# Where the magnitudes of a soft threshold lie: two PSUM banks for them, or a third pair of banks for the inverse beside them

## The chip, the cores and the metric

One core of a Trainium2 chip runs the whole program in one launch. The metric is the device time in microseconds, median of several runs; a profile of one execution stands beside it. The engines are TensorE (PE, with its weight loads as PEld), VectorE (DVE), ScalarE (ACT), GpSimd (POOL) and SyncE (SP), which issues the DMAs. Each engine works through its own queue in order.

## The reference

Four layers work on images x of shape (4, 64, 256, 256): batch, channels, rows, columns.

```python
# layers 0, 2 and 3: a long convolution with an implicit, separable filter
k_f = jnp.fft.rfft2(k, s=(512, 512)) / 512      # k = outer product of hx and hy, per channel
y = jnp.fft.irfft2(jnp.fft.rfft2(x, s=(512, 512)) * k_f, s=(512, 512))[..., :256, :256]
x = y + x * bias[:, None, None]
# layer 1: mixing of channels in the Haar domain, with a soft threshold
f1 = haar2d(x)
for i in range(2):
    f4 = jnp.einsum('bchw,oc->bohw', f1 * v[i], conv_w[i])
    acc = acc + jnp.sign(f4) * jax.nn.relu(jnp.abs(f4) - tau[i])
x = haar2d(acc, inverse=True) + x
```

The change is in layer 1's soft threshold: `jnp.abs(f4)` is the magnitude, `jnp.abs(f4) - tau` and the product with the sign are two VectorE operations on it.

## The kernel before

**Tiling.** The convolutions are done as products with Toeplitz matrices, rows first and then columns, in 64x64 tiles of TensorE (`toeplitz`, L337, its matmuls at L341). The Haar transform is partly a matmul with a 64x64 matrix (`haar`, L350, matmuls at L353) and partly sums and differences on GpSimd (`forward_free` and `inverse_free`, L430). The batch is cut in two groups of two images. A round t is a group and two channels; there are 32 rounds in a group and 64 in all.

**Stages.** `phase_a` does layer 0 and the forward transform. `phase_b(grp)` is the mixing of one group: for each of 64 steps two units u, one for each of the two terms i. `phase_c` does the inverse transform and layers 2 and 3. The order is written out by hand: each phase is a list of pieces, and `beside(main, side, ...)` (L1017) issues the pieces of one list spread evenly over those of another. The first mixing (group 0) goes beside `phase_a`'s second half, the second mixing (group 1) beside `phase_c`'s first 29 rounds; the rest of `phase_c`, the last stage, runs alone. The engines keep the order in which the pieces were issued, and semaphores settle the rest.

**A unit of the mixing** (L732): `mix` (L654) multiplies into the PSUM tile f4, named f in the profile; `multiply` (L673, DVE) takes it times v into the SBUF tile x; `sign` (L679, ACT) gives m; `magnitude` (L688, ACT) the absolute value; `less` (L693, DVE) subtracts the threshold; `threshold` (L698, DVE) takes the larger of that and 0 times the sign; `add` (L713 to L717, POOL) sums up into gt. In the second mixing every second unit from step 2 on is "raw": `multiply` only copies f4 out (L670) and the last stage's `shrink` (L829 to L855) thresholds it there.

**A round of the inverse** (`phase_c`'s `piece`, L950) has 18 pieces: rows of layer 2 (c1r), an inverse product (c0ps), columns of layer 3 of two rounds back (c2c), rows of layer 3 of the round before (c2r), another product (c0ps), columns of layer 2 (c1c). Each of them multiplies into a pair of PSUM banks from `banks` (L138), which goes around the list `rings`; a pair of the rows and columns serves two pieces, a pair of the product one. ACT copies c1r, c2r (L914) and c0ps (L902) out, DVE copies c1c and c2c with the residual (L933). These copies are issued by `flush` at the start of the piece that follows.

**PSUM** has 8 banks. In the first mixing: `acps` 4 (two pairs), f4 2, magnitude a 2. In the second mixing: `acps` 4, `wide2` 2 (a third pair), f4 2, while the magnitude overwrites x in SBUF. In the last stage: `acps` 4, `wide2` 2, the shrink tile x 2.

Of the kernel before, what the change touches and what calls it, by code (L numbers as in the profile page):

```python
# [41 lines left out]
F32 = mybir.dt.float32  # L42
AF = mybir.ActivationFunctionType
ALU = mybir.AluOpType
PSUM = bass.MemoryType.PSUM
DRAM = bass.MemoryType.DRAM

P = 128
# [19 lines left out]
GROUPS = 2  # L68
NB = B // GROUPS
# [15 lines left out]
W = 2 * N  # L85
# [16 lines left out]
def conv_haar_kernel(  # L102
# [19 lines left out]
    def pool(name, bufs, stack=ctx, **kw):  # L122
        return stack.enter_context(tc.tile_pool(name=name, bufs=bufs, reuse_waits="tile", **kw))

    ac = pool("ac", 2)
    acps = pool("acps", 4, space=PSUM)
# [8 lines left out]
    rings = [acps]  # L135
# [433 lines left out]
    def phase_b(grp):  # L569
# [4 lines left out]
        def raw(u):  # L574
            return grp == GROUPS - 1 and u % 2 == 1 and FULL <= u // 2 < STEPS
        st = [dict() for _ in range(STEPS)]
        un = [dict() for _ in range(units)]
# [103 lines left out]
        def magnitude(u):  # L681
            if raw(u):
                return
            if grp == GROUPS - 1:
                un[u]["a"] = un[u]["x"]
            else:
                un[u]["a"] = bps.tile([P, NB, W], F32, tag="a", name=f"a_{grp}_{u}", bufs=1)
            nc.scalar.activation(un[u]["a"], un[u]["x"], AF.Abs)  # L688

        def less(u):  # L690
# [41 lines left out]
        def piece(u, j):  # L732
# [13 lines left out]
            elif j == 1:  # L746
                if 0 < u <= units and grp < GROUPS - 1:
                    less(u - 1)
                if u + 1 < units and grp < GROUPS - 1:
                    mix(u + 1)  # L750
                if u < units:
                    sign(u)
                if i and s < STEPS and grp == GROUPS - 1:
                    store_raw(s)
                if 0 < u <= units:
                    threshold(u - 1)
                if i == 0 and s > 0:

                    load_v(s + 2)
                    if grp < GROUPS - 1:  # L760
                        load_f(s + 3)
            else:
                if u + 1 < units and grp == GROUPS - 1:
                    mix(u + 1)
                if i and s > 0 and grp == GROUPS - 1:
                    load_f(s + 3)
                if u < units:
                    magnitude(u)
                if i == 0 and s < STEPS:
                    exchange(s)  # L770
# [246 lines left out]
    def beside(main, side, lead, tail, weights=(1,)):  # L1017


        weights = [weights[k % len(weights)] for k in range(len(main))]  # L1020
        all_of = sum(weights[lead : len(main) - tail])
        done = 0
        for k, p in enumerate(main):
            p()
            want = len(side) * sum(weights[lead : k + 1]) // max(1, all_of)
            for q in side[done:want]:
                q()
            done = max(done, want)
# [10 lines left out]
    bps = pool("bps", 2, during, space=PSUM)  # L1039
# [3 lines left out]
    a = a[-2 * A_PIECES :]  # L1043
# [5 lines left out]
    beside(a_last[:1] + c_loads[1:] + a_last[1:] + c_first + a_end[:1], c_sums[half_way:], 2, 3)  # L1049
    during.close()  # L1050
    bp = pool("b2", 2, during)
    rings[:] = [acps, acps, pool("wide2", 2, space=PSUM)]
    bps = pool("bps2", 2, during, space=PSUM)

    main = c[:BLOCKS] + c[mid:C_PIECES] + a_end[1:] + c[BLOCKS:mid] + c[C_PIECES:cut_c]
    beside(main, phase_b(1), len(a_end) - 1 + 2 * BLOCKS, 0)
    during.close()
    late["sb"] = pool("late", 1)
    late["ps"] = pool("late_ps", 1, space=PSUM)
    beside(c[cut_c:], [], 0, 0)  # L1060
# [123 lines left out]
```

## Time and profile before

| what | before |
|---|---|
| median of three runs | 2478.4 us (2474.0 to 2486.93) |
| the profiled execution | 2475.7 us, span 2473.9 us |
| busy: PE, PEld, DVE, ACT, POOL | 91%, 76%, 72%, 56%, 84% of the span |
| first mixing, matmuls of L654 | 414 to about 1000 us |
| second mixing, matmuls of L654 | 1085 to 1762 us |
| last stage, alone | about 1770 us to the end |

A line of the groups view gives line, engine, operation, out<-in, shapes and count, then total busy time in us and the mean of one in ns, then the idle time of the engine just before them and what ended it. A line of the waits view gives who waited for whom: us in total, times, longest. A line of the timeline gives start and duration in us, engine, line and operation. A line of the table by stage gives the stretch and its length, then the busy time of PE, PEld, DVE, ACT and POOL with their instructions, the granted PE clock, the share of DMA and GB/s.

### The profile page before, as it was taken

What the parts mean: (1) busy time and instruction counts of PE and PEld (TensorE: products, weight loads), DVE (VectorE), ACT (ScalarE), POOL (GpSimd) and SP (SyncE); (2) the same over time, 40 slices, a digit from 0 to 9 for tenths busy, and PEclk for the clock granted to TensorE, in tenths of its full rate; (3) what the DMA queues carried; (4) which work ended last, traced back from release to release, by engine and by line L of the source; (5) the groups of instructions that cost most, each with busy time, mean ns of one, the idle gap of its engine ahead of it and who ended that gap; (6) DMA issues with size and microseconds to landing.
All of it is one profiled execution on the core that took longest, in us unless ns stands there. A gap on an engine that the chain in (4) does not pass through costs nothing.

```text
span 2473.9 us, 119298 instructions
## 1 busy us (share of the span) xinstructions
PE 2260.7 (91%) x53298; PEld 1883.8 (76%) x53298; DVE 1791.3 (72%) x1959; ACT 1392.7 (56%) x2318; POOL 2066.2 (84%) x2412
## 2 busy tenths in 40 slices
PE   7999998777777777778999999999999999999999
PEld 5779997444444444556887878888899999999998
DVE  4533335999999999768777777777577777777763
ACT  1232223677777777355666666666565555655552
POOL 2988887899999999777877878777889999999990
PEclk9999999999999999888999999999999999999999
DMA  6788888899999999557999999998866666666642
GB/s 198 246 279 303 295 306 302 285 350 354 359 336 359 354 344 338 208 200 276 328 316 327 330 326 334 334 334 312 282 221 218 211 214 212 218 215 212 219 166 102
DMA packets 222969, 688.03 MB, mean 278 GB/s; under 512 B 31470, under 2 KB 32815, under 8 KB 218232
## 3 DMA queue, kind: packets, MB, share of 16 engines
q1 hardware_dynamic: 222456, 680.40, 78.5%
q8 instruction: 419, 6.86, 1.1%
q14 instruction: 94, 0.77, 0.1%
HBM read 428.16 MB, written 252.12 MB: 275 GB/s over the span
## 4 chain that ended last, share of the span: by engine, by line
PE 46%; DVE 4%; DMA 2%; ACT 2%; issue 1%; SPq 1%; DVEq 0%; ACTq 0%
PE c2c L341 10%; PE c2r L341 10%; PE c1c L341 10%; PE c1r L341 9%; PE c0ps L353 4%; PE f L654 4%; DMA g<-mixed 1%; DVE x L693 1%; DVE cy L933 1%; DVE m L698 1%; DMA toep<-filt 1%; DVE x L673 1%; DMA rows<-in_v_rows 0%; ACT ch L914 0%; DVE o L933 0%
## 5 line engine op out<-in xcount | busy, mean ns | idle before, releaser
L430 POOL TENSOR_TENSOR i<-i,g 128x16 f32<-128x16 f32 x744 | 442.8, 616 | 27.2
L654 PE MATMUL f<-ft,mix 64*64 64x512 f32 x2048 | 306.8, 616 | 123.8 <-DVE x L673 109.4
L341 PEld LDWEIGHTS a2ps<-toep,ay 64*64 64x64 f32 x8192 | 303.7, 136 | 117.1 <-DVE f L522 53.2
L341 PE MATMUL a2ps<-toep,ay 64*64 64x128 f32 (+3 forms) x8192 | 336.9, 303 | 24.0 <-DVE f L522 20.6
L341 PEld LDWEIGHTS c1c<-toep,ch 64*64 64x64 f32 x8192 | 315.8, 133 | 42.9 <-issue 10.5
L341 PEld LDWEIGHTS c2c<-toep,ch 64*64 64x64 f32 x8192 | 306.5, 133 | 42.8 <-issue 12.5
L341 PEld LDWEIGHTS a1ps<-toep,x 64*64 64x64 f32 x8192 | 284.3, 134 | 58.9 <-issue 34.0
L341 PE MATMUL c1c<-toep,ch 64*64 64x256 f32 (+3 forms) x8192 | 323.0, 297 | 5.5 <-ACT ch L914 3.3
L341 PEld LDWEIGHTS c2r<-toep,cy 64*64 64x64 f32 x8192 | 300.8, 134 | 27.6 <-issue 13.9
L341 PE MATMUL c2r<-toep,cy 64*64 64x256 f32 (+3 forms) x8192 | 317.5, 297 | 4.4 <-issue 4.0
L341 PE MATMUL c1r<-toep,z 64*64 64x256 f32 (+3 forms) x8192 | 316.4, 297 | 5.4 <-issue 3.4
L430 POOL TENSOR_TENSOR ci<-i,g 128x1024 f32<-128x1024 f32 x124 | 315.7, 2566 | 4.5
L341 PE MATMUL a1ps<-toep,x 64*64 64x128 f32 (+3 forms) x8192 | 314.2, 298 | 5.7 <-DMA toep<-filt 2.4
L341 PEld LDWEIGHTS c1r<-toep,z 64*64 64x64 f32 x8192 | 298.3, 133 | 27.5 <-issue 11.2
L341 PE MATMUL c2c<-toep,ch 64*64 64x256 f32 (+3 forms) x8192 | 315.7, 297 | 3.0 <-issue 2.6
L679 ACT ACTIVATE m<-x 128x1024 f32<-128x1024 f32 x194 | 206.0, 1062 | 160.3 <-DVE x L673 122.1
L716 POOL TENSOR_TENSOR gt<-m,ft 128x512 f32<-128x512 f32 x128 | 164.5, 1285 | 152.7 <-DVE m L698 135.4
L489 ACT COPY ay<-a1ps 128x512 f32<-128x512 f32 x256 | 137.3, 589 | 269.2 <-PE a1ps L341 268.6
L914 ACT COPY ch<-c2r 128x512 f32<-128x512 f32 x256 | 137.2, 590 | 255.0 <-PE c2r L341 254.7
L673 DVE TENSOR_TENSOR x<-f,v 128x1024 f32<-128x1024 f32 x192 | 233.4, 1215 | 30.8 <-PE f L654 29.8
L509 DVE SCALAR_TENSOR_TENSOR x<-x,bias_sb,a2ps 128x512 f32<-128x512 f32 x256 | 179.5, 742 | 92.6 <-POOL f L391 51.3
L914 ACT COPY ch<-c1r 128x512 f32<-128x512 f32 x256 | 137.5, 594 | 167.1 <-PE c1r L341 166.7
(86 smaller groups left out, 3992.7 us busy)
## 6 DMA issues: line engine op xcount, KB each, us to landing
toep<-filt SPq DMA_DIRECT2D x768, 112.0 KB
ft<-coef SPq DMA_DIRECT2D x128, 512.0 KB
mixed<-gt SPq DMA_DIRECT2D x128, 512.0 KB
g<-mixed SPq DMA_DIRECT2D x256, 256.0 KB
x<-in_x SPq DMA_DIRECT2D x128, 256.0 KB
coef<-f SPq DMA_DIRECT2D x128, 256.0 KB
x<-in_x SPq DMA_DIRECT2D x32, 1024.0 KB
v<-in_v SPq DMA_DIRECT2D x64, 512.0 KB
```

Source lines behind the costliest of these rows:

```text
L341: nc.tensor.matmul(ps[r][half(c), j % 2, k * ROW :], data[half(r), c, k, bass.ts(j, ROW)], t(r, c)[:, : N - k * ROW], start=k == 0, stop=k ...
L353: nc.tensor.matmul(ps[r][half(c)].rearrange("p h k -> p (h k)"), matrix[half(r)], pairs(r, c).rearrange("p h k -> p (h k)"), start=True, s ...
L430: engine.tensor_tensor(to, s, d, op)
L489: later(lambda y=y, ps=ps: nc.scalar.copy(y, ps))
L509: nc.vector.scalar_tensor_tensor(to, old, bias_sb[:, c : c + 1], ps, ALU.mult, ALU.add)
L654: nc.tensor.matmul(un[u]["f4"][half(q), b, :], mixers[0][half(r), bass.ts(i, C)], st[s]["f"][half(r), b], start=True, stop=True, tile_posi ...
L673: nc.vector.tensor_tensor(un[u]["x"], un[u]["f4"], both(u, "v"), ALU.mult)
L679: nc.scalar.activation(un[u]["m"], un[u]["x"], AF.Sign)
L693: nc.vector.tensor_tensor(un[u]["a"], un[u]["a"], both(u, "tau"), ALU.subtract)
L698: nc.vector.scalar_tensor_tensor(un[u]["m"], un[u]["a"], 0.0, un[u]["m"], ALU.max, ALU.mult)
L716: nc.gpsimd.tensor_tensor(g[:, 0], m[:, 0], st[s]["f"][:, 0], ALU.add)
L914: later(lambda y=y, ps=ps: nc.scalar.copy(y, ps))
```

## The change

The magnitude of the second mixing is written to a PSUM tile `a` of its own, with one buffer, as in the first mixing. Its two banks are those of `wide2`: the inverse's ring has only `acps` (two pairs) while the second mixing runs, and gets `wide2` once the mixing's pools are closed, when the last stage begins.

```diff
         def magnitude(u):
             if raw(u):
                 return
-            if grp == GROUPS - 1:
-                un[u]["a"] = un[u]["x"]
-            else:
-                un[u]["a"] = bps.tile([P, NB, W], F32, tag="a", name=f"a_{grp}_{u}", bufs=1)
+            un[u]["a"] = bps.tile([P, NB, W], F32, tag="a", name=f"a_{grp}_{u}", bufs=1)
             nc.scalar.activation(un[u]["a"], un[u]["x"], AF.Abs)
...
     during.close()
     bp = pool("b2", 2, during)
-    rings[:] = [acps, acps, pool("wide2", 2, space=PSUM)]
     bps = pool("bps2", 2, during, space=PSUM)

     main = c[:BLOCKS] + c[mid:C_PIECES] + a_end[1:] + c[BLOCKS:mid] + c[C_PIECES:cut_c]
     beside(main, phase_b(1), len(a_end) - 1 + 2 * BLOCKS, 0)
     during.close()
+    rings[:] = [acps, acps, pool("wide2", 2, space=PSUM)]
     late["sb"] = pool("late", 1)
```

## The prediction

> **What bounds the kernel now.** I read the page first (TensorE, PE, 91% busy), then the table by stage, because the change touches one stage only: the second mixing, which runs beside the first rounds of the inverse (group 0). The matmuls of the mixing (L654) begin at 1085 us and end at 1762; the inverse starts at about 1053.
>
> ```profile
> 1053.00:1085.00 32.00, 20.70 (x412) 13.76 (x412) 17.42 (x23) 13.07 (x29) 30.36 (x47) 0.88 0.62 221
> 1085.00:1150.00 65.00, 55.07 (x1134) 41.94 (x1138) 53.90 (x47) 37.60 (x62) 43.82 (x38) 0.87 0.61 205
> 1150.00:1770.00 620.00, 602.27 (x14278) 516.88 (x14274) 459.31 (x439) 410.98 (x719) 479.85 (x522) 1.00 0.92 325
> 1770.00:2474.00 704.00, 694.33 (x18983) 658.83 (x18975) 483.55 (x548) 384.39 (x728) 596.60 (x598) 1.00 0.61 203
> ```
>
> The columns are length, then busy time of PE, weight loads, VectorE (DVE), ScalarE (ACT) and GpSimd (POOL), clock, DMA share, GB/s. In 1150 to 1770, PE is busy 602 of 620 us (97%), DVE 74%, ACT 66%, POOL 77%. So **PE sets the pace**: time freed on DVE or POOL is worth only what it takes out of PE's few gaps, and a new stall of PE counts in full. Next I asked what PE still waits for from 1053 to 1770, and the waits view names these as the largest that another engine causes (matmuls first, then weight loads; single waits of the start-up, for ft and cy, left out):
>
> ```profile
> PE f L654 <- DVE x L673: 8.4, 8, 1.6
> PE c1c L341 <- ACT ch L914: 3.3, 2, 3.0
> ...
> PEld f L654 <- DVE x L673: 11.3, 8, 3.1
> PEld c1c L341 <- ACT ch L914: 6.4, 10, 3.1
> PEld c2c L341 <- ACT ch L914: 4.3, 10, 0.8
> ```
>
> Weight load and matmul wait together, so the two kinds of rows overlap and I do not add them: about 11 us for f4 and 11 for the copies (6.4 + 4.3). Waits named "issue", some 54 us of weight-load waits in the same stretch (12.2, 11.6, 9.8, 9.6, 9.0, 2.2), have no releaser in the profile; I leave them alone. What DVE loses shows in the groups of the mixing, first the second mixing (1085 to 1770), then the first (410 to 1000):
>
> ```profile
> L698 DVE SCALAR_TENSOR_TENSOR m<-x,m 128x1024 f32<-128x1024 f32 x66 | 107.6, 1630 | 4.9
> L693 DVE TENSOR_TENSOR x<-x,v 128x1024 f32<-128x1024 f32 x64 | 98.1, 1533 | 7.8 <-ACT x L688 7.5
> ```
>
> ```profile
> L693 DVE TENSOR_TENSOR a<-a,v 128x1024 f32<-128x1024 f32 x128 | 157.1, 1227 | 7.2 <-ACT a L688 7.2
> L698 DVE SCALAR_TENSOR_TENSOR m<-a,m 128x1024 f32<-128x1024 f32 x127 | 155.5, 1225 | 14.2 <-DVE a L693 0.5 <-POOL f L391 0.5
> ```
>
> Same operations, same shapes: 1630 and 1533 ns with the magnitude in SBUF, 1225 and 1227 with it in PSUM.
>
> **What the Trainium skill says.** "SBUF — State Buffer", section "SBUF: two separate sides": VectorE and GpSimd share a port pair under an exclusive lock; a VectorE operation with two SBUF inputs and a GpSimd operation that reads SBUF shut each other out for a whole instruction. The trace agrees: only the rows with two SBUF inputs are stretched. "ScalarE: Activation LUTs", section "Step-by-step: what each stage is for": ScalarE writes PSUM faster than SBUF; L688 has a median of 1028 ns into PSUM and 1059 into SBUF. "VectorE: DVE Perf Modes", section "The perf-mode tier table (the rule you actually need)": an fp32 tensor_tensor runs at 1x from SBUF as from PSUM, so the PSUM operand itself should cost nothing; the shortest L693 in SBUF is 1207 ns, against 1227 on average in PSUM. "PSUM — Partial Sum Buffer", section "Terms": 8 banks of 2 KiB. A magnitude tile of 2 x 512 fp32 is 4 KiB, two banks, just what the third pair holds.
>
> **Part 1, the magnitude in PSUM.** 66 L698, 64 L693, and two L693 listed separately (4.8 us) fall to 1225: 107.6 + 98.1 + 4.8 - 132 x 1.225 = 49 us less on DVE. The 66 L688 save 66 x 31 ns = 2 us on ACT. No instruction is added, no DMA moves, SP's and POOL's queues keep their order. POOL loses the opposite waits: ci<-i,g took 2755 ns on average here, 2387 at its median over the kernel, so 54 x 0.37 = 20 us on this group alone. None of this lies on the path except through PE's 22 us of waits above. POOL is waited for by PE for under 2 us. From both sides: the gain is 0 to 22 us; I take **10**, since about half of those waits have a stretched instruction ahead of them at most.
>
> One wait is added: the magnitude tile has one buffer, so ACT's Abs of one shrunk unit waits until DVE's threshold of the shrunk unit before it. Behind it on ACT stand the exchange copies and the inverse's copies. From the third step on every second unit is not shrunk, so four side pieces, at 384 side pieces in 685 us some 7 us, lie between: no wait. Only the first four units are shrunk one after the other; the first mixing shows that case (L688 waits for m L698 114.5 us, 80 times, 1.4 each): at most 4 x 1.4 = 6 us, at a start-up where ACT waits for DVE anyway. I take 0.
>
> **Part 2, two pairs instead of three.** A round of the inverse uses ten pairs of banks: c1r, c1r, c0ps, c2c, c2c, c2r, c2r, c0ps, c1c, c1c. Today a pair is needed again three pairs later, then two. The rule I read off the timeline: is the last copy out of pair k-2 over when the first matmul of pair k starts today? One stretch, with all three engines:
>
> ```profile
> 1432.04 1.13 PE L353 MATMUL c0ps<-ci,inverse_sb 64*64 64x512 f32 x8
> 1432.90 3.50 PE L341 MATMUL c1c<-toep,ch 64*64 64x256 f32 x91
> 1433.50 6.80 POOL L430 TENSOR_TENSOR ci<-i,g 128x1024 f32<-128x1024 f32 x2
> 1434.08 1.07 ACT L914 COPY ch<-c2r 128x512 f32<-128x512 f32 x2
> 1434.85 3.21 DVE L698 SCALAR_TENSOR_TENSOR m<-x,m 128x1024 f32<-128x1024 f32 x1
> 1437.98 2.71 DVE L933 SCALAR_TENSOR_TENSOR cy<-z,bias_sb,c1c 128x512 f32<-128x512 f32 x4
> 1438.12 0.38 PE L341 MATMUL c1r<-toep,z 64*64 64x256 f32 x1
> ```
>
> c1c starts at 1432.90; the second c2r pair, two before it with only the 1.1 us inverse product between, is emptied by 1434.08 + 1.07 = 1435.15: 2.25 us late. c1r starts at 1438.12; the first c1c pair is empty only after two of the four cy copies, 1437.98 + 1.4 = 1439.4: 1.3 late. The second delay has a stretched threshold ahead of it (3.21 instead of 1.22); the first has not, it is ACT's queue.
>
> Done for every pair: from 1150 to 1770, 100 of 253 are late, 125.8 us in all: c2r to c1c 34.0, c1c to c1r 30.6, c1r to c2c 25.9, c0ps to c2c 11.2, c0ps to c1c 10.7, c2c to c2r 7.2, c1r to c0ps 5.9, rest 0.3. From 1053 to 1150, 18 of 32, 30.5 us. A delay shifts what follows, so these must not simply be added. Walking in order, with a running shift, gives two ends. If a copy keeps its distance from its last matmul (its queue shifts with PE), 95 + 22 = **117 us**. If a copy keeps its own time unless PE itself is later (its queue had other work anyway), 17 + 10 = **27 us**. The first mixing, which has two pairs already, lies between: PE waits there for DVE f (46.6), ACT ay (38.2) and ACT f (4.4) at its weight loads, 89 us of them over 155 pairs, but 30 of them (17.0, 10.4, 2.8) at the matmuls; 30/155 x 285 pairs = 55 us. I take **52** for the loss, near this and below the middle of 27 and 117 (72), since PE's present gaps swallow some of it.
>
> **Part 3, from the last stage on.** Three pairs again, and the banks of f4 and a pass to the third pair and the shrink tile. The order is unchanged; the new wait is for the last raw copy and threshold, which end at 1763.4 and 1767.0, while c1c of the next round starts at 1770.2. Cost 0; without that cover, one DVE copy, 1.2 us. The chain at 1773 to 1791 runs over DMA (rows, raw), unchanged.
>
> **Sum.** +52 - 10 = +42. The profiled execution took 2475.7 us (span 2473.9), 2.7 below the median 2478.4. On its own time: 2475.7 + 42 = **2518**.
>
> **The rivals.** (1) The lock was the real cost: copies come sooner because DVE and POOL stop blocking each other, and ACT waits less for x L673 (103.5 us today). Then the loss is at its low end and the gain at its high end: 27 - 22 = +5; should the freed queues also remove most of the 27 (say all but 7), -15: 2461, **faster**. It decides where the copies' delays fall below about half of the low end. For it: 49 us of DVE and the 3.21 us example. Against: 88 of the 126 us lie behind pairs that ACT empties (c2r, c1r and c0ps: 34.0 + 25.9 + 11.2 + 10.7 + 5.9 + 0.3), and ACT's own work hardly shrinks. (2) Loss and gain cancel, 2464 to 2488: needs the low end with a gain of 15 or more. (3) The pessimistic end: 117 - 10, 2583, if every queue shifts with PE. (4) The change does nothing because the third pair was hardly used: excluded, 100 of 253 pairs use it.
>
> **How the numbers follow.** A measurement of this kernel can tell about 0.5%, 12 us, from no change. Chances: main forecast with (3), slower by more: 0.78; (2) 0.10; (1) 0.12. The range 2470 to 2578 leaves out the end of (1) and the last of (3).
>
> **What would show it.** Right: L693 and L698 in the second mixing at about 1225 ns, PE and its weight loads waiting at c1c, c2c and c1r for ACT ch, ACT z and DVE cy, tens of us in total; PE below 95% busy in a second mixing that ends 30 to 60 us later; the last stage as long as before. Wrong: PE at 97% or more there with few such waits, or L693/L698 still above 1500.

## The result and the profile after

The changed kernel took **2500.6 us** (median of 4 runs, 2498.7 to 2500.8) against 2477.8 us before (now four runs): 23 us slower, ratio 1.0097 with a 95% interval of 1.0075 to 1.0118. The profiled execution took 2500.8 us, its span 2499.1. The forecast was 2518, range 2470 to 2578, slower.

The table by stage of the changed kernel, columns as before; the cuts follow its own stages (it began 2 us later):

```profile
1055.00:1087.00 32.00, 22.18 (x414) 14.92 (x412) 16.30 (x20) 13.35 (x30) 30.35 (x47) 0.89 0.61 220
1087.00:1152.00 65.00, 58.75 (x1211) 48.57 (x1215) 49.23 (x53) 37.32 (x63) 37.34 (x42) 0.92 0.68 228
1152.00:1798.00 646.00, 621.83 (x14195) 531.08 (x14189) 414.14 (x435) 406.46 (x718) 432.63 (x520) 0.99 0.88 310
1798.00:2499.00 701.00, 693.42 (x19000) 661.40 (x18991) 481.21 (x548) 384.29 (x728) 597.04 (x597) 1.00 0.62 203
```

The whole difference lies in the third row, the second mixing: 646 us where it was 620. DVE has 45 us and POOL 47 us less to do there, and yet the stage is longer. The busy share of PE does not show a loss of 26 us: 96% where it was 97%, and in microseconds PE is counted as busy for longer (622 us where it was 602, for about as many matmuls). Nor does the granted clock explain it: the four runs of the changed kernel were granted 0.984 to 0.988 and lie within 2.1 us of each other; 32 runs of the kernel before were granted 0.982 to 0.987, no more. Where PE is held up shows in what its weight loads wait for, from 1053 to 1798:

```profile
PEld c1c L341 <- ACT ch L911: 34.3, 42, 4.7
PEld c2c L341 <- ACT ch L911: 22.8, 35, 2.2
...
PEld c2r L341 <- issue: 8.0, 17, 1.3
PEld c1r L341 <- DVE cy L930: 7.5, 7, 4.8
PEld c2r L341 <- DVE o L930: 4.4, 10, 0.6
PEld c1r L341 <- issue: 4.0, 6, 1.4
```

c1c and c2c now wait 57 us for ScalarE's copies, where it was 11. Two waits have shrunk. The mixing's wait for x (11.3 us before) is gone. And the waits named "issue" are 20.0 us in all (8.0, 4.0, 3.0, 1.9, 1.8, 1.3), where they were 54.

These rows must not be added up to a loss. A weight load can wait while the matmuls ahead of it still run, and most of this waiting is of that kind: at the matmuls themselves the copies ch are named for 18.3 us (3.3 before) and "issue" for 5.8 (8.0 before). Another part of a stall stands in the profile as busy time. The longest matmuls of c1c, which wait for these copies, before (1152 to 1770 us) and after (1152 to 1798):

```profile
L341 PE MATMUL c1c<-toep,ch 64*64 64x256 f32 x800 | 83.1, 380 | 4.0 <-ACT ch L914 3.3 <-issue 0.5
```

```profile
L341 PE MATMUL c1c<-toep,ch 64*64 64x256 f32 x800 | 94.3, 399 | 13.1 <-ACT ch L911 13.1
```

800 matmuls of the same shape take 399 ns on average instead of 380; those of c1r, which hardly wait, stay at 377 and 378. So the waits say where PE is held up, and the times of the runs say what it costs.

The groups of the second mixing on VectorE, which took 1630 and 1533 ns before:

```profile
L695 DVE SCALAR_TENSOR_TENSOR m<-a,m 128x1024 f32<-128x1024 f32 x65 | 79.4, 1222 | 4.9
...
L690 DVE TENSOR_TENSOR a<-a,v 128x1024 f32<-128x1024 f32 x63 | 77.0, 1223 | 1.6 <-ACT a L685 1.4
```

So both halves of the change did what they say. One stall in full, in the timeline of the changed kernel, at the place that the prediction took as its example (the second c2r pair, the product, then c1c):

```profile
1440.82 1.02 ACT L685 ACTIVATE a<-x 128x1024 f32<-128x1024 f32 x1
1440.97 1.13 PE L353 MATMUL c0ps<-ci,inverse_sb 64*64 64x512 f32 x8
...
1441.86 1.24 ACT L701 COPY other<-ft 64x512 f32<-64x512 f32 x2
...
1443.13 1.07 ACT L911 COPY ch<-c2r 128x512 f32<-128x512 f32 x2
...
1443.77 0.20 PEld L341 LDWEIGHTS c1c<-toep,ch 64*64 64x64 f32 x4 [2.56 <-ACT ch L911]
1443.77 4.77 PE L341 MATMUL c1c<-toep,ch 64*64 64x256 f32 x70 [1.67 <-ACT ch L911]
```

The product ends near 1442.1. c1c needs the two banks of c2r, whose copies start at 1443.13, because the magnitude (1.02 us) and the exchange (1.24 us) stand ahead of them on ScalarE. PE's weight loads wait 2.56 us, its matmuls 1.67: for the rest of the 2.56 the product was still running.

### The profile page after: what moved, and what is told of

It reads as the page before. It is cut to its first block, busy times and chain, and to the rows that moved or that the text cites. A ratio compares the mean times of both kernels' runs of the same rounds, so it can differ in the third digit from the quotient of the medians.

```text
span 2499.1 us, 119347 instructions
## 1 busy us (share of the span) xinstructions
PE 2285.6 (91%) x53298; PEld 1898.1 (76%) x53298; DVE 1738.1 (70%) x1959; ACT 1388.1 (56%) x2318; POOL 2013.6 (81%) x2412
## 4 chain that ended last, share of the span: by engine, by line
PE 47%; ACT 3%; DMA 2%; DVE 2%; issue 1%; SPq 1%; DVEq 0%; ACTq 0%
PE c1c L341 11%; PE c2c L341 10%; PE c2r L341 10%; PE c1r L341 9%; PE c0ps L353 4%; PE f L654 4%; ACT ch L911 1%; ACT other L701 1%; DMA g<-mixed 1%; ACT a L685 1%; ACT g L407 0%; DVE a L690 0%; SPq L164 0%; DMA rows<-in_v_rows 0%; DVE cy L930 0%
## 5 line engine op out<-in xcount | busy, mean ns | idle before, releaser
L430 POOL TENSOR_TENSOR i<-i,g 128x16 f32<-128x16 f32 x744 | 426.6, 594 | 27.2
L341 PE MATMUL c1c<-toep,ch 64*64 64x192 f32 (+3 forms) x8192 | 327.4, 301 | 13.5 <-ACT ch L911 13.1
L341 PE MATMUL c1r<-toep,z 64*64 64x192 f32 (+3 forms) x8192 | 321.8, 299 | 10.1 <-issue 4.1
L341 PEld LDWEIGHTS c1r<-toep,z 64*64 64x64 f32 x8192 | 307.4, 134 | 27.7 <-DVE cy L930 7.5
L341 PE MATMUL c2r<-toep,cy 64*64 64x128 f32 (+3 forms) x8192 | 323.4, 298 | 4.0 <-issue 3.0
L341 PE MATMUL c2c<-toep,ch 64*64 64x128 f32 (+3 forms) x8192 | 319.8, 297 | 6.8 <-ACT ch L911 5.5
L341 PE MATMUL a1ps<-toep,x 64*64 64x256 f32 (+3 forms) x8192 | 314.7, 299 | 5.1 <-DMA toep<-filt 2.6
L430 POOL TENSOR_TENSOR ci<-i,g 128x1024 f32<-128x1024 f32 x124 | 294.1, 2393 | 4.5
L673 DVE TENSOR_TENSOR x<-f,v 128x1024 f32<-128x1024 f32 x192 | 233.6, 1217 | 45.7 <-PE f L654 43.7
L685 ACT ACTIVATE a<-x 128x1024 f32<-128x1024 f32 x194 | 199.1, 1026 | 117.3 <-DVE m L695 117.3
L695 DVE SCALAR_TENSOR_TENSOR m<-a,m 128x1024 f32<-128x1024 f32 x194 | 237.4, 1224 | 19.2 <-POOL f L391 0.5
```

The lines of the kernel that those rows point to most:

```text
L341: nc.tensor.matmul(ps[r][half(c), j % 2, k * ROW :], data[half(r), c, k, bass.ts(j, ROW)], t(r, c)[:, : N - k * ROW], start=k == 0, stop=k ...
L430: engine.tensor_tensor(to, s, d, op)
L673: nc.vector.tensor_tensor(un[u]["x"], un[u]["f4"], both(u, "v"), ALU.mult)
L695: nc.vector.scalar_tensor_tensor(un[u]["m"], un[u]["a"], 0.0, un[u]["m"], ALU.max, ALU.mult)
```

## The experiments

Each run after the first is timed against 11 to 32 runs of the kernel before on the same chip. "us" beside a ratio is what it differs from 1, times 2477. Kernels that leave work out ("no lock", "no exchange") are there for their time alone.

| run | ratio | 95% interval | us |
|---|---|---|---|
| the change | 1.0097 | 1.0075 to 1.0118 | +24 |
| ring half alone | 1.0189 | 1.0164 to 1.0213 | +47 |
| five banks, magnitude in SBUF | 1.0107 | 1.0084 to 1.0131 | +27 |
| change, copies split | 1.0072 | 1.0053 to 1.0092 | +18 |
| two pairs in the last stage | 1.0439 | 1.0410 to 1.0468 | +109 |
| three pairs, no lock | 0.9933 | 0.9913 to 0.9953 | -17 |
| two pairs, no lock | 1.0097 | 1.0076 to 1.0117 | +24 |
| three pairs, copies split | 0.9986 | 0.9975 to 0.9997 | -3.5 |
| five banks, magnitude in one | 1.0034 | 1.0022 to 1.0047 | +8 |
| change, no exchange | 1.0025 | 1.0013 to 1.0038 | +6 |
| three pairs, no lock, rounds 6 on | 0.9956 | 0.9940 to 0.9971 | -11 |
| two pairs, no lock, rounds 6 on | 1.0107 | 1.0086 to 1.0129 | +27 |

**The ring half alone.** The third pair moved to the last stage; the magnitude stays over x in SBUF.

```diff
-    rings[:] = [acps, acps, pool("wide2", 2, space=PSUM)]
     bps = pool("bps2", 2, during, space=PSUM)
...
     during.close()
+    rings[:] = [acps, acps, pool("wide2", 2, space=PSUM)]
```

> Only the ring half of the change: two pairs of banks beside the second mixing, three from the last stage on, the magnitude still in SBUF over x. Theory A (the missing third pair costs, the freed VectorE/GpSimd lock gives some 10 us back): slower than before by 33 us, that is about 10 us slower than the changed kernel; L693 and L698 stay at 1.5 to 1.6 us, weight loads wait for ACT ch at c1c and c2c by 50 us or more. Rival B (the loss comes from the magnitude in PSUM: its single buffer and the wait of ACT for it): within 5 us of before. Rival C (the lock has no value to TensorE): the same as the changed kernel, +23.

Median 2521.95 us, +47 by the ratio. So the ring costs 47 us and the magnitude in PSUM gives 23 of it back: B falls, C falls, and A holds in direction, but its "10 us" is too small. L693 and L698 stay at 1615 and 1519 ns. The weight loads (1053 to 1815 us) say where the lock costs:

```profile
PEld c1c L341 <- ACT ch L914: 35.0, 45, 3.6
PEld c2c L341 <- ACT ch L914: 23.6, 34, 2.6
PEld c1r L341 <- DVE cy L933: 22.3, 27, 6.4
```

The first two are nearly those of the changed kernel (34.3 and 22.8). The third is 22.3 us where the change has 7.5: copies on VectorE that stand behind a held-up L693 or L698. In the kernel before, this wait does not stand among its waits at all, because there a third pair covers it. And the mixing's wait for x, 11.3 us before, is gone here too, although L693 and L698 are as slow as before: the ring half is enough to take it away.

**Five banks.** Single banks in turn, so one comes back after two and a half pairs. The stages before and after take their banks one by one too, but still have as many; the last stage lasts as long as before (713 and 712 us from the start of the mixing's last matmul).

```diff
-        ring = rings[asked[0] % len(rings)]
-        asked[0] += 1
-        return [ring.tile([P, 2, N], F32, tag="ps", name=f"{name}_{r}") for r in range(2)]
+        def one(r):
+            ring = rings[asked[0] % len(rings)]
+            asked[0] += 1
+            return ring.tile([P, 2, N], F32, tag="ps", name=f"{name}_{r}")
+
+        return [one(r) for r in range(2)]
...
-    rings[:] = [acps, acps, pool("wide2", 2, space=PSUM)]
+    rings[:] = [acps] * 4 + [pool("extra", 1, during, space=PSUM)]
...
```

> Magnitude in SBUF as before, but the ring beside the second mixing has five single banks instead of six (every tile takes the next bank), so a bank comes back after two and a half pairs. Theory A: the loss of the ring grows as the distance of reuse shrinks; the same walk through the trace of before, per bank, gives 17 to 80 us where it gave 27 to 117 for four banks, so some 60% of what the four-bank ring costs: +15 to +22 us. Rival D (only a whole third pair in flight helps, since both banks of a pair are needed together): as slow as four banks, +30. Rival E (the loss sits at the two boundaries of the stage): under +5.

Median 2501.2 us, +27: 57% of what four banks cost. The loss goes with the distance of reuse, bank by bank; E falls, and D too: its +30 lies inside the interval (+21 to +32), but four banks cost 47. (The +15 to +22 was 60% of an assumed 25 to 37; the share was right, the base too small.)

**Copies split between two engines**, on the changed kernel.

```diff
-                    later(lambda y=y, ps=ps: nc.scalar.copy(y, ps))
+                    copy = nc.vector.tensor_copy if r and t < ROUNDS - AHEAD else nc.scalar.copy
+                    later(lambda y=y, ps=ps, copy=copy: copy(y, ps))
```

> The changed kernel, with the second of the two copies out of each c1r and c2r pair on VectorE instead of ScalarE in the rounds beside the second mixing (some 112 copies; the first copy stays on ScalarE). Theory A: the waits of c1c and c2c for ACT ch (57 us of weight loads) come from two copies of 0.59 us one after the other behind a product that lasts 1.1 us; side by side they end 0.5 us sooner, 56 times, so 15 to 25 us come back and the time is near that of before (2476 to 2486). Rival F (the copies are late because of what stands ahead of them in the queues, and VectorE's queue is no shorter): within 5 us of the changed kernel, or slower.

Median 2492.9 us, 6 us less by the ratios (with both intervals between 1 more and 13 less) where 15 to 25 were expected. Weight loads, 1053 to 1790 us:

```profile
PEld c1c L341 <- ACT ch L912: 23.7, 19, 3.8
PEld c2c L341 <- ACT ch L912: 14.7, 14, 2.3
...
PEld c1c L341 <- issue: 10.7, 24, 2.3
...
PEld c2c L341 <- DVE ch L912: 6.7, 6, 1.3
PEld c1c L341 <- DVE ch L912: 5.6, 5, 2.2
```

The waits of c1c and c2c for both engines' copies are 51 us, not 57: 44 of them where there were 77, but longer ones on average. And "issue" rose from 20 to 33 us. A's size misses by more than half; F's "within 5 us" is neither met nor excluded. It may be that most of the lateness stands ahead of the copies, which the next run tests.

**What stands ahead on ScalarE.** The changed kernel without the exchange.

```diff
         def exchange(s):
+            if grp == GROUPS - 1:
+                st[s]["other"] = st[s]["f"][:, 1]
+                return
```

> The changed kernel without the exchange copies of the second mixing: ScalarE's two copies per step (L701 other<-ft, 126 of 0.62 us, 78 us of its queue) are left out and GpSimd adds ft itself, so half of the second mixing's sum takes the wrong partitions. Theory A, as corrected by the split copies (8 of an expected 15 to 25 us): the copies of c1r and c2r are late by what stands ahead of them on ScalarE as well as by their own 1.2 us; with 1.25 us less ahead in every second unit, the waits of c1c and c2c for ACT ch fall from 57 to some 35 us and 5 to 12 us come back. Rival L (only their own length counts): within 3 us of the changed kernel.

Median 2484.4 us, 18 us less than the change, more than the 5 to 12 expected; L falls. The two rows to set beside 34.3 and 22.8:

```profile
PEld c1c L341 <- ACT ch L914: 26.7, 45, 2.2
PEld c2c L341 <- ACT ch L914: 14.5, 31, 1.9
```

Nearly as many waits, but shorter. So with two pairs PE pays for the queue ahead of the copies. Whether it pays more for that than for the copies' own length is not shown: the split copies took their place in VectorE's queue, where c1c and c2c then waited 12 us for them.

**Two pairs in the last stage.** The kernel before with `rings[:] = [acps]` from there on.

> The kernel before, but with two pairs of banks in the last stage (three beside the second mixing as before). This asks whether the walk through the trace sizes such a loss where nothing else is changed: for 1770 to 2474 us it gives 48 us (copies keep their own time) to 160 us (copies keep their distance from their last matmul). Theory A: +50 to +90, nearer the low end, and the second mixing unchanged. Rival G (without the mixing's f4 the copies are always in time): under +15.

Median 2586.5 us, +109, and the second mixing's last unit starts as before, within the 6 us by which this execution was late already at its first unit. G falls; the size lies above A's 50 to 90, though between the two ends of the walk (48 and 160). The waits of the weight loads from 1770 us on name 140 us of it:

```profile
PEld c1c L341 <- ACT ch L914: 81.6, 68, 2.3
PEld c2c L341 <- ACT ch L914: 58.4, 70, 2.7
```

Here the walk's middle (104) was right. Beside the second mixing the ring's 47 lie below the middle of 27 and 117.

**The lock by itself.** GpSimd's inverse beside the second mixing becomes a memset, which reads no SBUF; at three pairs and at two.

```diff
-                if engine is nc.gpsimd:
+                if zero:
+                    engine.memset(to, 0.0)
+                elif engine is nc.gpsimd:
...
-                s["ops"] = inverse_free(s["g"], s["ci"], f"i{t}_", nc.vector if t < 2 else nc.gpsimd, levels(t))
+                s["ops"] = inverse_free(s["g"], s["ci"], f"i{t}_", nc.vector if t < 2 else nc.gpsimd, levels(t), 2 <= t < ROUNDS - 1)
```

> The kernel before (three pairs, magnitude in SBUF), with GpSimd's sums and differences of the inverse (L430) replaced by a memset of the same output in rounds 2 to 30, those beside the second mixing: GpSimd reads no SBUF there, so L693 and L698 cannot be held up by it. The inverse of these rounds is left out (zeros go on). After the first experiments the two halves of the change measure +45 (ring) and about -22 (magnitude in PSUM, at two pairs). Theory A (the 22 us come from copies on VectorE that stand behind a held-up instruction while TensorE waits for their banks, so they are worth much less when a third pair covers the copies): L693 and L698 at 1.22 us, and 0 to 11 us faster than before. Rival H (the lock costs TensorE the same whatever the ring): 20 us or more faster.

> The same memset in place of L430 in the kernel with only the ring half of the change (two pairs, magnitude in SBUF, +45): the inverse of rounds 2 to 30 is left out. Theory A (the gain of the magnitude in PSUM is the lock between VectorE and GpSimd, nothing else): as fast as the changed kernel, +23, 2500, with c1r's waits for DVE cy falling from 21 to about 8 us. Rival I (it comes from ScalarE's faster write into PSUM, or from x being free sooner): stays above +38.

At three pairs 2460.0 us, -17, outside both answers. At two pairs 2497.7 us, +24, the changed kernel's ratio (to the last digit by chance: the intervals are 5 us to either side), and 23 us less than the ring half alone: I falls. c1r waits 4.6 us for DVE cy there, where the ring half alone has 22.3. The groups of the two-pair run, with the magnitude in SBUF:

```profile
L700 DVE SCALAR_TENSOR_TENSOR m<-x,m 128x1024 f32<-128x1024 f32 x66 | 81.6, 1237 | 4.8
...
L695 DVE TENSOR_TENSOR x<-x,v 128x1024 f32<-128x1024 f32 x64 | 77.9, 1217 | 1.1 <-ACT x L690 1.0
```

1237 and 1217 ns: from SBUF they are nearly as fast as from PSUM (1222 and 1223), once GpSimd's inverse reads nothing (its sums of the mixing still read SBUF). This agrees with "SBUF — State Buffer", section "SBUF: two separate sides", in the Trainium skill, which makes the lock on a VectorE operation with two SBUF inputs a matter of GpSimd operations that read SBUF. The memset also makes GpSimd's own work shorter, so the savings of these runs are bounds from above on what the lock costs. To part the start-up, where the lock holds operations that the change leaves in SBUF, from the steady stage, the same with the memset from about 1160 us on:

> The kernel before with GpSimd's L430 a memset in rounds 6 to 30 only, that is from about 1160 us on; the inverse of these rounds is left out. With rounds 2 to 30 it was 17 us faster than before, but by the times of the mixing's units in its profile about 11 of these came before 1185 us, in the start-up, where the lock also holds the 64x512 operations of the first two steps, which the change leaves in SBUF. Theory A (with three pairs the lock is worth little once the stage runs steadily): 1 to 6 us faster than before. Rival H (it is worth some 15 us in the steady stage too): 12 us or more faster.

> The same memset in rounds 6 to 30 with only the ring half of the change (two pairs, magnitude in SBUF, +45 us). Theory A (with two pairs the copies on VectorE stand on the path, so the lock counts in the steady stage): 15 to 22 us faster than that kernel, so +23 to +30 against before. Rival M (its value is in the start-up at two pairs as well): +38 or more.

At three pairs 2467.7 us, -11 (interval -15 to -7): between A's 1 to 6 and H's 12, so my reading of the start-up out of one profile took too much for it. At two pairs 2504.4 us, 20 us less than the ring half alone: M falls. The wait for DVE cy fell with it, from 22.3 us to 10.7:

```profile
PEld c1r L341 <- DVE cy L935: 10.7, 9, 6.4
```

So the lock is worth some 11 us at most in the steady stage with three pairs and 20 with two. The intervals of these differences are some 4 and 8 us to either side, so the times alone don't prove that the second is larger. The waits speak for two different costs: with three pairs it is the mixing's wait for x (11.3 us before, 3.4 with this memset), with fewer it is c1r's wait for DVE cy (22.3 us with two pairs, 14.1 with five banks, none with three).

**Divisions that keep more.** First the kernel before with the copies split as above:

> The kernel before with the second copy out of each c1r and c2r pair on VectorE in the rounds beside the second mixing, as in the earlier run on the changed kernel, which took 8 us off it. Theory A (with a third pair the copies are mostly in time: weight loads wait for ACT ch 12 us only): within 5 us of before, rather slower, since VectorE's queue holds held-up instructions. Rival J (moving work off ScalarE pays by itself): 8 us faster than before.

Median 2470.9 us, ratio 0.9986 (0.9975 to 0.9997): 3.5 us faster than before, the fastest of the kernels that leave nothing out, though by less than 0.5%. A expected within 5 us and rather slower; J's 8 us did not come. "Issue" waits of the weight loads from 1053 to 1770 us are 73 us there (16.5, 14.9, 14.8, 12.8, 11.1, 2.6), where the kernel before had 54. The waits for copies of c1r and c2r fell by less, from 11 us to 6, so where these come from is not shown.

Then five banks, and one bank for the magnitude, in two halves:

```diff
...
+        def half_threshold(u, b):
+            if not 0 <= u < units or raw(u):
+                return
+            h, m = un[u]["h", b], un[u]["m"][:, b]
+            nc.vector.tensor_tensor(h, h, st[u // 2]["tau"][u % 2], ALU.subtract)
+            nc.vector.scalar_tensor_tensor(m, h, 0.0, m, ALU.max, ALU.mult)
...
```

> A division of the 8 banks between the two kernels: beside the second mixing a ring of five single banks, and one bank for the magnitude, which is made, lessened and thresholded in two halves of 512 columns (132 more instructions on VectorE of about 0.15 us each, 20 us, and 66 on ScalarE). Five banks with the magnitude in SBUF took +24. Theory A: the lock is worth something between its value at two pairs (22) and at three (0 to 11), so +8 to +16. Rival K (the extra instructions eat it): +20 or more.

Median 2484.5 us, +8, 18 us less than five banks with the magnitude in SBUF; K falls. It is faster than the change but not than before: for these two banks the inverse is the better user.

## Why the prediction was right, and where its numbers were off

- **PE sets the pace** held. 92 us of DVE and POOL time went away in the mixing (45 + 47 in the table) and the stage grew by 26. That a new stall "counts in full" did not: the ring half alone has some 75 us more waits of weight loads for copies (48 for ACT ch, 22 for c1r's DVE cy, 5 for DVE o), less the 11 us of f4's wait for x, and costs 47.
- **The ring's loss** was put at 52 between 27 and 117 and measures 47 (41 to 53). The kinds of pairs were right too: c1c behind c2r and c2c behind c1r, with only the product between, make up the waits for ACT ch, and c1r behind c1c those for DVE cy. That 52 came so close is partly luck. It was taken from the waits at matmuls of the first mixing; by the same measure the ring half alone has 33 us of waits for copies against 12 before, only some 22 more. And the place between the walk's two ends differs from run to run: about a fifth of the way up for four and five banks, over half of it for the last stage (109 between 48 and 160).
- **The gain was mis-sized**: 10 of a bound 0 to 22, measured 23 (15 to 31). The failed step is the one that sized it by PE's waits in the kernel before ("None of this lies on the path except through PE's 22 us of waits above"). That reads the worth of the lock with three pairs, where the runs give about 11. But the two halves of the change are made together. The ring half alone already removes the 11 us of f4's wait for x, half of that bound. In its place c1r waits 22.3 us for the copies cy on VectorE and for the held-up instructions ahead of them, and the magnitude in PSUM brings this to 7.5. The example of the prediction, a threshold of 3.21 us ahead of four cy copies, showed it; outside rival (1) it was booked only under the loss.
- **The sum**, +42 against +23 (medians), is off by those two terms, 5 us of loss and 13 of gain: 42 - 18 = 24.
- **PE's present gaps swallow some of it** is not shown. The "issue" waits of the weight loads fell from 54 to 20 us, but most of them lie behind matmuls that still run; at the matmuls they are 8.0 and 5.8. One of the 54, of 6.6 us, is the start-up stall that the rows of the matmuls lay to DVE cy, so it does have a releaser.
- **The signs.** L693 and L698 at 1225 ns and the waits at c1c, c2c and c1r came as described. Two others were just missed: PE below 95% busy (it is 96%; part of a stall is counted as busy), and a second mixing that ends 30 to 60 us later (its last matmul begins at 1789 us where it was 1762, 28 later).
- **The added wait for the magnitude's one buffer** was put at 0 and is 3.0 us on ACT, in two waits at the start-up (1105 and 1110 us). **The last stage** was put at 0; 701 us against 704 in the tables.
- Rival (1), the lock as the real cost, was right on what the lock is and wrong on the balance: 23 is half of 47.

What stays open: what the "issue" waits are, where they do not lie behind running matmuls, and how much of a stall the profile counts as busy time.

## What to carry to other kernels

When two edits trade one resource between two users, price each with the other already made: a delay that a spare buffer hides costs little until the buffer is taken. For a ring of buffers, ask of each reuse which is the shortest piece of work that the copy out must fit behind, and what else stands ahead of that copy in its engine's queue. An engine that is already busy 97% of a stage gives back only part of what others are freed of (23 us for 92 here), and the waits of its weight loads say where it is held up, not how much time is lost: some 75 us of new waits cost 47 us beside the mixing, 136 us cost 109 in the last stage.

## What the runs showed of the hardware that was not expected

Lost time of PE need not show as idle time. From the start of the inverse to the end of the second mixing PE is counted as busy 678 us in the kernel before and 703 us in the changed kernel, for nearly as many matmuls (15,820 and 15,812), while its idle time is 39 and 40 us.

Waits of weight loads that the profile lays to nothing ("issue") are not a constant of the program: 54 us before, 20 us with two pairs of banks, 33 with two pairs and split copies, 73 with three pairs and split copies, for nearly the same matmuls in the same stage. At the matmuls they are 8.0, 5.8, 8.9 and 13.3 us.

The prediction said that only VectorE operations with two SBUF inputs are stretched. One with a single SBUF input was too: in the start-up, L639 (a multiplication by a constant, 64x512) took 2.58 us beside GpSimd's inverse and 0.41 beside the memset, and the like L641 took 0.42 in the kernel before.
